# Seven of eight sequences send their tokens to two experts through rows in memory ordered by expert

## The chip, the cores and the metric

The kernel runs on one core of a Trainium2 chip. The core has TensorE (matrix products), VectorE (DVE), ScalarE (ACT), GpSimd (POOL) and SyncE (SP, which only issues transfers here). Each engine works through its own instructions in order and waits on semaphores for the others. The metric is the device time of one execution in microseconds. The kernel before takes 966.37 us, the median of three runs (964.07 to 969.08).

## The reference

The input is x with 8 sequences of 512 tokens of 256 values, all in float32. The first half is an attention of 16 heads plus a memory term, the second a mixture of experts; each is added to its input and normalised.

```python
x = L0_attn_x
x = _layernorm(x + _L0_attn_ref(x, ...), axis=-1)
x = _layernorm(x + _L0_ffn_ref(x, ...), axis=-1)
```

The second half picks for each token the 2 best of 10 experts. Eight are real and two are null (they contribute nothing). The reference computes all eight experts for every token and weighs them, six or more with zero:

```python
gate_probs = jax.nn.softmax(x @ gate_w.T + gate_b, axis=-1)
weights, selected = jax.lax.top_k(gate_probs, 2)
true_weights = weights * (selected < 8)
norm_w = true_weights / where(sum(true_weights) > 0, sum(true_weights), 1)
combine_w = einsum('tk,tke->te', norm_w, one_hot(selected, 10))[:, :8]
expert_out = einsum('td,edh->teh', x, expert_w) + expert_b
out = einsum('te,teh->th', combine_w, expert_out)
```

## The kernel before

A sequence's 512 tokens are four tiles of 128. The program is written out by a planner in Python, before the chip sees it; what the chip executes is a fixed order on every engine.

The backbone is a loop over 32 attention units (sequence b, group g of four heads). Each unit has eight turns. A turn emits score products (`products`, L174): the row maxima need one pass (TensorE L184 and L191, VectorE L194), the scores another (L188), followed by the exponential on ScalarE (L197), a causal selection on GpSimd (L199) and, two turns later, the value products (`values`, L214, TensorE L220). The tile of the maxima's scores has one buffer, so the next one waits until VectorE has reduced the last. A unit begins with the transpose L206.

After its backbone part every turn calls `fill` (L755). It has a credit of TensorE time and spends it on generators: *chains*, which may advance up to twice a turn, and *bulk* work, taken while credit is left. A `yield` of a number is a cost in microseconds; `STEP` goes on at the next turn; `POOL` lets only one chain use GpSimd in a turn; a lambda waits until a condition of the planner holds. All of this is decided while the program is written.

The work put between the attention turns is: the memory term (`lines`, `memory_sums`, until about a third of the span); then for each sequence a front (L597) and its experts (`all_experts`, L691). `prepare` (L551), the first part of a front, loads x again (L558), adds the output's bias and the memory's share on GpSimd, loads the inverted denominators of attention (L571) and multiplies by them (L577). The denominators travel by memory: L230 writes them, L239 reads them in another shape, L243 writes the inverse. `front` then does the output products (L606, L609), the normalisation, the transposes (L629), the gate (L635) and the choice of experts on VectorE with small operations. `all_experts` computes all eight experts for each tile, two at a time:

```python
for k in range(KC):
    nc.tensor.matmul(pe, x1T[:, k, c * P : (c + 1) * P],
                     ws[:, k, 2 * ep : 2 * ep + 2, :].rearrange("p e h -> p (e h)"), ...)   # L707
for e in range(2):
    nc.vector.scalar_tensor_tensor(x1[:, c, :], pe[:, e * D : (e + 1) * D], cw[...], x1[:, c, :], ALU.mult, ALU.add)  # L711
```

Then come the bias by one product (L715), its addition (L716) and the second normalisation, and each tile is stored (L723). Fronts are one chain (`fronts`, L729), so preparation of sequence b+1 starts after front b; a front also waits for experts of earlier sequences (`b < left[0] + 2`, L624), and preparation for a free buffer of x (`b < left[0] + 4`, L552). x transposed lies in on-chip memory for all eight sequences (L85). At the end `fill` is called until everything has been emitted.

Of the kernel before, what the change touches and what calls it, by code (L numbers as in the profile page):

```python
# [27 lines left out]
EARLY, MORE = 0.6, 0.9  # L28
PV, PQ, PO = 1.2, 2.15, (1.05, 0.85, 0.65, 0.45)
ROUNDS = (2, 1, 1, 1)  # L30
AHEAD = 5
HALF = 4
# [35 lines left out]
def block_kernel(ctx, tc, x, xT, wqk, bqk, wtok, wod, memv, memvb, row, gw, we, eb, out):  # L68
# [14 lines left out]
    xt = const.tile([P, B, KC, T], F32, name="xt")  # L83

    def load_xT(b):  # L85
        nc.sync.dma_start(xt[:, b], xT[b].rearrange("(k p) t -> p k t", p=P))
# [4 lines left out]
    load_xT(0)  # L91
# [15 lines left out]
    ebs = const.tile([NTRUE, D], F32, name="ebs")  # L107
# [6 lines left out]
    for b in range(1, B):  # L114
        load_xT(b)
    gws = const.tile([P, KC, NE], F32, name="gws")
    nc.sync.dma_start(gws, gw.rearrange("(k p) e -> p k e", p=P))

# [12 lines left out]
    nc.gpsimd.iota(first, pattern=[[-1, NE]], base=NE, channel_multiplier=0,  # L131
                   allow_small_or_imprecise_dtypes=True)
# [18 lines left out]
    def project_qk(u, w):  # L151


        b, g = UNITS[u]
        pq = bank(f"pq{u}_{w}")
        for k in range(KC):
            nc.tensor.matmul(pq, wq[:, k, w, g // 2, :], xt[:, b, k, :], start=(k == 0), stop=(k == KC - 1))  # L157
        for odd in range(2):
            t = att.tile([P, T], F32, name=f"qk{u + odd}_{w}", tag=f"qk{w}", bufs=4)
            n = NG * w + g + odd  # L160
            nc.scalar.activation(t, pq, AF.Identity, bias=bq[:, n : n + 1], scale=bq[:, 2 * NG + odd : 2 * NG + odd + 1])  # L161
            qk[u + odd, w] = t

    def project_v(b, c):
        pv = bank(f"pv{b}_{c}")
        for k in range(KC):
            nc.tensor.matmul(pv[:, :D], xt[:, b, k, c * P : (c + 1) * P], wt[:, k, CV : CV + D],  # L167
                             start=(k == 0), stop=(k == KC - 1))
        nc.scalar.copy(v_aug[b % 2][:, c, :, 0::2], pv[:, :D].rearrange("p (h q d) -> p h q d", q=2, d=DH))
# [84 lines left out]
    def fold_values():  # L254
# [22 lines left out]
        nc.sync.dma_start(ebs, eb)  # L277
# [6 lines left out]
    def memory():  # L284
        with tc.tile_pool(name="lines", bufs=2) as lp:
            lines_pool.append(lp)
            spawn(memory_factors())
            spawn(fold_values())
            for b in range(B):
                half = b // HALF  # L290
                if b % HALF == 0:


                    t, keep = mem.setdefault(half, {}), memp if half else lp
                    t["rd"] = keep.tile([P, NT, H, HALF, 6], F32, name=f"rd{half}", bufs=1)
                    t["jw"] = keep.tile([P, NT, H, HALF, 7], F32, name=f"jw{half}", bufs=1)
                    t["rn"] = memp.tile([P, NT, H, HALF], F32, name=f"rn{half}", tag="rn", bufs=2)
                    t["gexp"] = memp.tile([P, NT, H, HALF], F32, name=f"gexp{half}", tag="gexp", bufs=2)
                yield lambda: b < 2 or b - 2 in turned
                yield from lines(lp, b)  # L300
            yield lambda: B - 1 in lined and finished.count(0) == 2
        lines_over.append(True)
# [8 lines left out]
    def lines(lp, b):  # L311
# [4 lines left out]
        for c in range(NT):  # L316
            pl = bank(f"pl{b}_{c}")
            for k in range(KC):
                nc.tensor.matmul(pl[:, : CW - CL], xt[:, b, k, c * P : (c + 1) * P], wt[:, k, CL:CW],  # L319
# [180 lines left out]
    def finish(half, h0, rm):  # L500
        yield STEP
        yield lambda: half == 0 or half - 1 in gates
# [48 lines left out]
    def prepare(b):  # L551
        yield lambda: lines_over and b < left[0] + 4  # L552
# [4 lines left out]
        xb = st[b]["xb"] = ff.tile([P, NT, D], F32, tag="x1", name=f"x1_{b}", bufs=4)  # L557
# [39 lines left out]
    def front(b):  # L597

        yield from prepare(b)
        ff, osb, xb = ffp[0], st[b]["osb"], st[b]["xb"]  # L600
        y = xb
        mv = ff.tile([P, NT, 2], F32, tag="mv", name=f"mv1_{b}")
        for c in range(NT):
            pa = bank(f"pa{b}_{c}")
            for k in range(KC):
                nc.tensor.matmul(pa[:, D:], xt[:, b, k, c * P : (c + 1) * P], wt[:, k, CM : CM + D],  # L606
# [8 lines left out]
            yield 1.9  # L615
        yield STEP
        x1 = y
# [6 lines left out]
        yield lambda: b < left[0] + 2  # L624
        x1T = ff.tile([P, KC, T], F32, tag="x1T", name=f"x1T_{b}")
# [28 lines left out]
        for r in range(2):  # L654
# [6 lines left out]
            oh = small(f"oh{r}", NE)  # L661
# [16 lines left out]
        w = small("w", NE)  # L678
        nc.vector.tensor_tensor(w, hot[0], hot[1], ALU.add)
        nc.vector.tensor_tensor(w, w, ex, ALU.mult)  # L680
        yield STEP
        dn = small("dn")
        nc.vector.tensor_reduce(dn, w[:, :, :NTRUE], AX.X, ALU.add)  # L683
        nc.vector.scalar_tensor_tensor(dn, dn, 0.0, dn, ALU.is_equal, ALU.add)
        nc.vector.reciprocal(dn, dn)
        cw = ff.tile([P, NT, NTRUE], F32, tag="cw", name=f"cw_{b}")
        nc.vector.tensor_tensor(cw, w[:, :, :NTRUE], bc(dn, 2, NTRUE), ALU.mult)
        st[b].update(x1=x1, x1T=x1T, cw=cw)
        ready.add(b)

    def all_experts(b):  # L691
# [10 lines left out]
        mv2 = ff.tile([P, NT, 2], F32, tag="mv", name=f"mv2_{b}")  # L702
        for c in range(NT):
# [11 lines left out]
            nc.tensor.matmul(pb[:, :D], cT[:, c * P : (c + 1) * P], ebs, start=True, stop=True)  # L715
# [9 lines left out]

    def fronts():  # L729
        for b in range(B):  # L730
            yield from front(b)

    def tiles():
        for b in range(B):
            yield from all_experts(b)

    left = [0]
# [17 lines left out]
    def fill(need, most=3.0):  # L755
        credit[0] = min(credit[0] + need + (MORE if ready else EARLY), most)
# [22 lines left out]
    for n in range(B // HALF):  # L779
        spawn(memory_ahead(n))  # L780
    spawn(fronts())

    done, credit = set(), [0.0]
    project_qk(0, 0)
# [3 lines left out]
    for u in range(-1, U + 1):  # L788
        b, g = UNITS[u] if 0 <= u < U else (0 if u < 0 else B, -1)
        for i in range(NT if u < U else 2):  # L790
            for pr in range(2):
                products(u, i, pr)
                need = TAKE[i]
# [27 lines left out]
    while chains or any(it[1] != "over" for it in bulk):  # L821
        fill(0.3)
# [60 lines left out]
```

## Time and profile before

| | us |
|---|---|
| median of 3 runs | 966.37 |
| the profiled execution | 966.05 |
| its span, first to last instruction | 964.2 |
| TensorE busy in the span | 885.6 |
| VectorE busy | 606.8 |
| ScalarE busy | 309.6 |
| GpSimd busy | 313.3 |
| start of attention unit 13 | 369.1 |
| start of attention unit 31, the last | 815.7 |

The profile records one execution. Busy times are unions of an engine's instructions; matmuls are pipelined, so their durations overlap and a mean is longer than what one more matmul costs. A float32 product appears as two MATMUL records. The granted clock of TensorE is 0.962 in the mean of the span, and 1.00 in the stretches after 369.1 us until the last 8 us.

### The profile page before, as it was taken

What the parts mean: (1) busy time and instruction counts of PE and PEld (TensorE: products, weight loads), DVE (VectorE), ACT (ScalarE), POOL (GpSimd) and SP (SyncE); (2) the same over time, 40 slices, a digit from 0 to 9 for tenths busy, and PEclk for the clock granted to TensorE, in tenths of its full rate; (3) what the DMA queues carried; (4) which work ended last, traced back from release to release, by engine and by line L of the source; (5) the groups of instructions that cost most, each with busy time, mean ns of one, the idle gap of its engine ahead of it and who ended that gap; (6) DMA issues with size and microseconds to landing.
All of it is one profiled execution on the core that took longest, in us unless ns stands there. A gap on an engine that the chain in (4) does not pass through costs nothing.

```text
span 964.2 us, 14019 instructions
## 1 busy us (share of the span) xinstructions
PE 885.6 (92%) x5360; PEld 426.0 (44%) x5360; DVE 606.8 (63%) x1293; ACT 309.6 (32%) x606; POOL 313.3 (32%) x501
## 2 busy tenths in 40 slices
PE   6999987888788899999999999999999999979996
PEld 3544443444354454354544344543444344334442
DVE  1234657886966656756766866556655676577765
ACT  4164633344324233333323333332333332200000
POOL 1067763536363422521153113211231124230000
PEclk9799988999889799999999999999999999999998
DMA  7300000000000000100100000000000010020000
GB/s 247 95 11 16 11 7 4 3 2 24 4 23 24 13 14 10 39 2 3 39 30 1 2 26 23 23 1 22 28 23 1 4 46 23 3 67 1 22 22 22
DMA packets 25459, 23.67 MB, mean 25 GB/s; under 512 B 8324, under 2 KB 21132, under 8 KB 25392
## 3 DMA queue, kind: packets, MB, share of 16 engines
q1 hardware_dynamic: 24288, 22.22, 7.2%
q8 instruction: 42, 0.69, 0.3%
q10 hardware_dynamic: 1056, 0.40, 0.2%
q0 software_dynamic: 48, 0.16, 0.1%
q14 instruction: 25, 0.20, 0.1%
HBM read 16.73 MB, written 4.73 MB: 22 GB/s over the span
## 4 chain that ended last, share of the span: by engine, by line
PE 69%; DVE 16%; POOL 6%; DMA 3%; issue 3%; ACT 2%; SPq 0%; POOLq 0%; DVEq 0%; ACTq 0%
PE pex L707 22%; PE mx L184 14%; PE po L220 5%; PE pq L157 5%; DVE negmax L194 5%; PE mx L191 4%; PE pa L606 3%; PE pa L609 3%; PE pv L167 2%; PE sc L188 2%; DVE x L711 2%; DMA s<-w 2%; PE pbias L715 2%; PE pm L475 1%; DVE pr L485 1%
## 5 line engine op out<-in xcount | busy, mean ns | idle before, releaser
L197 ACT ACTIVATE pe<-sc 128x1024 f32<-128x1024 f32 (+3 forms) x256 | 180.1, 704 | 415.6 <-PE sc L188 400.0
L194 DVE TENSOR_REDUCE negmax<-mx 128x2 f32<-128x256 f32 (+3 forms) x256 | 209.4, 818 | 154.3 <-PE mx L191 153.9
L184 PE MATMUL mx<-qk,qk 32*128 32x128 f32 (+3 forms) x1024 | 226.7, 500 | 48.3 <-DVE negmax L194 45.8
L199 POOL TENSOR_SCALAR_AFFINE_SELECT pe<-pe 128x256 f32<-128x256 f32 x256 | 104.6, 409 | 475.4 <-ACT pe L197 475.0
L707 PE MATMUL pex<-ws,x1T 128*128 128x512 f32 x512 | 242.1, 606 | 3.7 <-DVE dn L683 2.1
L188 PE MATMUL sc<-qk,qk 32*128 32x512 f32 (+3 forms) x1024 | 217.4, 497 | 2.4 <-ACT pe L197 1.2
L711 DVE SCALAR_TENSOR_TENSOR x<-pex,cw,x 128x256 f32<-128x256 f32 x256 | 123.5, 482 | 92.8 <-PE pex L707 86.8
L184 PEld LDWEIGHTS mx<-qk,qk 32*128 32x128 f32 x1024 | 86.5, 190 | 170.6 <-DVE negmax L194 93.1
L707 PEld LDWEIGHTS pex<-ws,x1T 128*128 128x128 f32 x512 | 90.7, 190 | 112.2 <-issue 104.2
L220 PE MATMUL po<-pe,v_aug 128*32 128x512 f32 (+3 forms) x1024 | 98.9, 459 | 0.0
L188 PEld LDWEIGHTS sc<-qk,qk 32*128 32x128 f32 x1024 | 81.8, 189 | 11.5 <-ACT pe L197 4.7
L191 PEld LDWEIGHTS <-identb 128*128 128x128 bf16 x512 | 29.3, 98 | 119.3 <-issue 112.1
L191 PE MATMUL mx<-mask_ts,identb 128*128 128x128 bf16 x512 | 74.9, 229 | 0.0
L157 PE MATMUL pq<-xt,wq 128*128 128x512 f32 x128 | 65.5, 638 | 5.9 <-DMA xt<-in_xT 5.9
L161 ACT ACTIVATE qk<-pq,bq 128x512 f32<-128x512 f32 x64 | 46.3, 773 | 31.6 <-PE pq L157 31.6
L475 PE MATMUL pm<-ou,dm 128*128 128x144 f32 x256 | 48.4, 320 | 1.6 <-DVE pr L485 1.6
L475 PEld LDWEIGHTS pm<-ou,dm 128*128 128x128 f32 x256 | 39.2, 208 | 17.3 <-issue 12.4
L446 POOL TENSOR_TENSOR ou<-jw,jf 128x288 f32<-128x288 f32 x64 | 43.7, 688 | 1.3
L167 PE MATMUL pv<-wt,xt 128*128 128x256 f32 x128 | 37.9, 423 | 0.0
L585 POOL TENSOR_TENSOR rr_b<-rs_b,half 128x4 f32<-128x4 f32 x8 | 8.1, 1006 | 90.3 <-DVE rs_b L583 90.3
L483 DVE SCALAR_TENSOR_TENSOR ou<-pm,last,ou 32x288 f32<-32x288 f32 x48 | 25.2, 525 | 18.8 <-POOL ou L446 12.8
L319 PE MATMUL pl<-wt,xt 128*128 128x272 f32 x128 | 36.6, 423 | 0.0
(162 smaller groups left out, 872.9 us busy)
## 6 DMA issues: line engine op xcount, KB each, us to landing
xt<-in_xT SPq DMA_DIRECT2D x8, 512.0 KB
x<-in_x SPq DMA_DIRECT2D x8, 512.0 KB
recs<-dr SPq DMA_DIRECT2D x16, 256.0 KB
out_y<-x SPq DMA_DIRECT2D x32, 128.0 KB
ws<-in_we SPq DMA_DIRECT2D x2, 1024.0 KB
s<-w SPq DMA_DIRECT2D x8, 127.0 KB
qk<-nt ACTq DMA_DIRECT2D x32, 8.0 KB
wq<-in_wqk SPq DMA_DIRECT2D x3, 128.0 KB
```

The source lines that it names most:

```text
L157: nc.tensor.matmul(pq, wq[:, k, w, g // 2, :], xt[:, b, k, :], start=(k == 0), stop=(k == KC - 1))
L167: nc.tensor.matmul(pv[:, :D], xt[:, b, k, c * P : (c + 1) * P], wt[:, k, CV : CV + D], start=(k == 0), stop=(k == KC - 1))
L184: nc.tensor.matmul(mx[:, h, :n], qk[m, 0][r, n - P : n], qk[m, 1][r, :n], start=True, stop=False)
L188: nc.tensor.matmul(sc[:, h, :n], qk[v, 1][r, j * P : (j + 1) * P], qk[v, 0][r, j * P :], start=True, stop=True)
L191: nc.tensor.matmul(mx[:, h, n - P : n], identb, mask_ts, start=False, stop=True)
L194: nc.vector.tensor_reduce(negmax[m][:, 2 * pr : 2 * pr + 2, t], mx[:, :, :n], AX.X, ALU.max, negate=True)
L197: nc.scalar.activation(pe[:, :, :n], sc[:, :, :n], AF.Exp, scale=DH**-0.5)
L199: nc.gpsimd.affine_select(out=pe[:, :, :P], in_=pe[:, :, :P], compare_op=ALU.is_ge, fill=0.0, base=0, pattern=[[0, 2], [1, P]], channel_mu ...
L220: nc.tensor.matmul(pos[u][32 * h : 32 * h + 32, j * P :], v_aug[b % 2][:, j, 4 * (g // 2) + h, g % 2 : g % 2 + 2].rearrange("p q d -> p (q ...
L475: nc.tensor.matmul(pm[:, i * HALF * 36 : (i + 1) * HALF * 36], dms[h + i], ou[:, i], start=True, stop=True)
L707: nc.tensor.matmul(pe, x1T[:, k, c * P : (c + 1) * P], ws[:, k, 2 * ep : 2 * ep + 2, :].rearrange("p e h -> p (e h)"), start=(k == 0), sto ...
L711: nc.vector.scalar_tensor_tensor(x1[:, c, :], pe[:, e * D : (e + 1) * D], cw[:, c, 2 * ep + e : 2 * ep + e + 1], x1[:, c, :], ALU.mult, AL ...
```

## The change

For sequences 0 to 6 the experts are no longer computed for all tokens. Each sequence has 1024 choices (two per token). They are given places in a row buffer in device memory, ordered by expert, where each expert's part is rounded up to whole tiles of 128 rows; at most 15 tiles result (8 plus 7 for rounding), and always 15 are worked through.

- `front` keeps, instead of a dense weight matrix, the two one-hot choices (`hot`), the two weights (`wr`), and running counts per expert (`to`, `had`).
- `sort` computes each choice's row: two small TensorE products give ranks and totals, small VectorE operations turn them into tile bases, row numbers `at` (a null expert gets a row past the end), and a table `tab` with the expert of each tile. GpSimd then scatters the tokens by 8 indirect transfers of 128 rows.
- `experts` fetches a tile of sorted rows on SP, transposes it on TensorE with a copy on ScalarE, multiplies by the weights of the expert whose number is loaded from `tab` into registers (for up to 4 tiles at once, on TensorE and VectorE), adds that expert's bias on VectorE, and stores the result to a second row buffer on SP.
- `combine` gathers each token's two result rows by 8 indirect transfers on GpSimd, adds them with their weights, normalises and stores the sequence by one transfer.
- Sequence 7 stays with `all_experts`; its biases are loaded into a small tile, since the biases of all experts now lie spread over 128 partitions.
- x transposed has five buffers; sequences 5 to 7 are loaded when needed, once for the memory's lines and again for attention. Row buffers (three of each kind) are cleared by transfers on SP during the early units.
- Preparation, fronts and reloading are chains of their own. A front waits until the tokens two sequences back have been scattered. The credit per turn after the first front is 0.8 instead of 0.9, and 1.1 instead of 0.3 after attention.

```diff
-EARLY, MORE = 0.6, 0.9
+EARLY, MORE = 0.6, 0.8
+DENSE = 1
+GROUPS = tuple((b,) for b in range(B - DENSE))
+MAXTILES = 8 * max(len(g) for g in GROUPS) + 7
+XT, X1 = 5, 4
...
+    def clear():
...
+        for i in range(3):
+            nc.sync.dma_start(ysl[i][NOROW:], nought[0:1])
+            for rows_of in (xsl[i], ysl[i]):
+                for n in range(0, MAXTILES, 4):
...
+                    nc.sync.dma_start(rows_of[...].rearrange("(n p) d -> p n d", p=P), bc(nought, 1, w))
+                    yield
...
     def front(b):
-        yield from prepare(b)
+        yield lambda: b in prepared and (b < 2 or 'sorted' in group[b - 2])
...
-        yield lambda: b < left[0] + 2
-        x1T = ff.tile([P, KC, T], F32, tag="x1T", name=f"x1T_{b}")
+        x1T = osb
...
+    def sort(p):
...
+        yield lambda: left[0] >= p - 2
+        pr = bank(f"rank{p}")
...
+        nc.tensor.matmul(pr[:, : (n + 1) * NTRUE], ones, gr["had"]..., start=True, stop=False)
+        nc.tensor.matmul(pr[:, : n * NTRUE], ahead, gr["to"]..., start=False, stop=True)
...
+        for c in range(n):
+            yield POOL
+            x1 = gr["x1"][c // NT][:, c % NT, :]
+            for r in range(2):
+                went = nc.gpsimd.indirect_dma_start(
+                    out=xsl[p % 3], out_offset=bass.IndirectOffsetOnAxis(ap=gr["at"][r][:, c : c + 1], axis=0),
+                    in_=x1, in_offset=None, bounds_check=NOROW - 1, oob_is_err=False).ins
...
+    def experts():
...
+                xs[n] = ffp[0].tile([P, D], F32, tag="xs", name=f"xs{p}_{t}", bufs=4)
+                load = nc.sync.dma_start(xs[n], xsl[p % 3][t * P : (t + 1) * P]).ins
...
+                nc.tensor.transpose(pt[:, k * P : (k + 1) * P], xs[n][:, k * P : (k + 1) * P], ident)
+            xT_s[n] = ffp[0].tile([P, KC, P], F32, tag="xTs", name=f"xTs{p}_{t}")
+            nc.scalar.copy(xT_s[n], pt[:, : KC * P]...)
...
+            if t % 4 == 0:
...
+                _, of_t = nc.values_load_multi_w_load_instructions(
+                    group[p]["tab"][0:1, t : t + w], engines=[mybir.EngineType.PE, mybir.EngineType.DVE], ...)
...
+                nc.tensor.matmul(py[:, :D], xT_s[n][:, k, :], ws[:, k, bass.ds(of[n], 1), :]..., ...)
+            ys = ffp[0].tile([P, D], F32, tag="ys", name=f"ys{p}_{t}", bufs=2)
+            nc.vector.tensor_tensor(ys, py[:, :D], ebs[:, bass.ds(of[n], 1), :]..., ALU.add)
+            nc.sync.dma_start(ysl[p % 3][t * P : (t + 1) * P], ys)
+            yield 1.1
...
+    def combine(p):
...
+                    nc.gpsimd.indirect_dma_start(
+                        out=y, out_offset=None, in_=ysl[p % 3],
+                        in_offset=bass.IndirectOffsetOnAxis(ap=gr["at"][r][:, n : n + 1], axis=0))
...
+            nc.sync.dma_start(out[b].rearrange("(c p) d -> p c d", p=P), x1)
+            left[0] += 1
...
     def tiles():
-        for b in range(B):
+        yield from experts()
+        for b in range(B - DENSE, B):
             yield from all_experts(b)
...
     while chains or any(it[1] != "over" for it in bulk):
-        fill(0.3)
+        fill(1.1)
```

## The prediction

> **What bounds the kernel now.** First the page's shares, then the groups of TensorE, then the busy time by stage, then the chain of waits at the end, then single rows of GpSimd.
>
> ```profile
> PE   885.6 (92%) x5360; PEld 426.0 (44%) x5360; DVE 606.8 (63%) x1293; ACT 309.6 (32%) x606; POOL 313.3 (32%) x501
> ...
> L707 PE MATMUL pex<-ws,x1T 128*128 128x512 f32 x512 | 242.1, 606 | 3.7 <-DVE dn L683 2.1
> L711 DVE SCALAR_TENSOR_TENSOR x<-pex,cw,x 128x256 f32<-128x256 f32 x256 | 123.5, 482 | 92.8 <-PE pex L707 86.8
> ```
>
> The experts' products (L707) are TensorE's largest group: 512 MATMUL records, 64 for each of eight sequences (an f32 product is two records). VectorE's adds of their results (L711) wait for TensorE, not the reverse. Next the same by stage; the columns are the stretch, its length, then busy microseconds of each engine.
>
> ```profile
> 42.90:369.10 326.20, 284.27 (x1977) 146.38 (x1976) 209.85 (x385) 135.35 (x298) 167.69 (x262) 0.92 0.04 12
> 369.10:815.70 446.60, 433.33 (x2824) 198.31 (x2822) 290.81 (x632) 149.02 (x249) 121.92 (x196) 1.00 0.06 19
> ```
>
> I cut the span at the 32 transposes L206, which begin an attention unit (four heads of one sequence). Units 13 to 30 fill 369.1 to 815.7 us: 24.8 us each, TensorE busy 97%. There a microsecond of TensorE work is worth nearly a microsecond. Earlier the memory arithmetic also holds TensorE back, and that is not changed. After the last unit begins (815.7), 148.5 us remain. The chain of waits there:
>
> ```profile
> 849.76 3.83 DMA x<-in_x
> ...
> 860.80 3.51 DMA recs<-dr
> ...
> 865.76 0.70 PE pa L609 x2
> 866.46 0.86 PE pa L606 x4
> ...
> 871.64 1.72 PE pex L707 x4
> 873.36 0.62 PE pbias L715 x2
> ...
> 892.24 0.45 PE px L629 x4
> ```
>
> The last front waits for its x, fetched as late as 849.8. These rows also give streaming prices, which I use in place of group means, since pipelined records overlap: a 512-column MATMUL 1.72/4 = 0.43 us, a 256-column one 0.86/4 = 0.215, a transpose 0.45/4 = 0.11, a bias product 0.31.
>
> **The change, part by part.**
>
> *Expert products.* Removed from a sequence: 64 x 0.43 = 27.5, eight bias records x 0.31 = 2.5, eight of L698 about 1.0 (as transposes): 31.0 us. Added: 15 tiles, each 4 records of 256 columns (0.86) and 4 transposes (0.44), so 19.6, and 0.2 for the ranks: 19.8. Net -11.2, for seven sequences **-78 us**. The ideal share of two experts in eight isn't reached: 15 tiles instead of 8, 256 columns instead of 512, and a second transposition. By the order of the changed program's instructions this falls about 2.5 before unit 13, 33 in units 13 to 30, and 43 after.
>
> *Chains of their own.* Preparation no longer stands inside the fronts, so x of sequence 7 is asked for some two units before the end of attention. In the stretch 846 to 866 TensorE is idle about 6 us before single instructions. **-6 us.**
>
> *Register loads.* Each group of up to four tiles loads its experts' numbers into registers of TensorE and VectorE: 28 loads on each, in order, so scores, projections and values queue behind. No row of before shows one. From below: nothing, if TensorE has enough queued work. From above: the Trainium skill, "Runtime: NRT & Kernel Launch", section Instruction fetch mechanics, puts a register load at about 200 ns per register, so an estimate of 0.8 us for four. I take 0.7 exposed: **+20 us**; ends 0 and, with 2 us each, 56. The first load also waits for all engines and most DMA queues: **+3** (near one 512 KB landing, 3.83). Register moves before each product (210) stand behind queued matmuls: 0.
>
> *Scatter and gather.* 16 indirect transfers for each of seven sequences, 112 on GpSimd's queue, in pairs, mostly one pair to a turn of the planner. The nearest row is a plain one of 128 rows:
>
> ```profile
> L95 POOL DMA_DIRECT2D rows<-in_row x1 | 0.8, 752 | 0.8 <-POOLq L871 0.8
> ...
> 747.22 0.41 POOL L199 TENSOR_SCALAR_AFFINE_SELECT pe<-pe 128x256 f32<-128x256 f32 x1 [4.07 <-ACT pe L197]
> 750.46 0.41 POOL L199 TENSOR_SCALAR_AFFINE_SELECT pe<-pe 128x256 f32<-128x256 f32 x1 [2.83 <-ACT pe L197]
> ```
>
> The row says 0.75 us; reading 128 indices comes on top, and I take T = 1.2. Against the change speaks the Trainium skill, "SBUF — State Buffer", section SBUF: two separate sides: a GpSimd DMA of some 620 ns took about 3100 beside a VectorE copy, because descriptors are written through the port pair shared with VectorE. Before has no such transfer beside VectorE work, but shows the lock's other side: a VectorE product of two SBUF operands, (3.6 - 2.2)/7 = 0.2 us in its other seven records, lasts as long as GpSimd's 2.36 us addition beside it.
>
> ```profile
> 853.92 2.22 DVE L680 TENSOR_TENSOR w<-w,ex 128x40 f32<-128x40 f32 x1
> ```
>
> What is queued behind a pair is the next causal selection (L199), and the value products (L220) wait for that. A turn is an eighth of a unit, about 3.05 us after; a pair and a selection take 2T + 0.41. With T = 1.2 that is 2.8 and nothing is late. Above 3.05 it lags in each of four consecutive turns. A selection ends about 4.8 us before its value product begins in this trace (median in units 13 to 30), so a group of four stalls TensorE by 4(2T - 2.64) - 4.8, and some 12 groups lie beside attention. By the row: 0. By the page's 3.1: 9.4 x 12 = 113 us. I take **0**; a gain is excluded, since nothing is removed here.
>
> *Transfers on SP.* 105 tile loads and 105 result stores at 0.33 to 0.45 us of issue: 80 us of SP, which only waits most of the time. A tile is fetched two turns (6 us) ahead, against 3.83 for a 512 KB landing: hidden. But the load of x for sequences 4 to 7 stands behind the store that frees its buffer, and tile transfers queue behind both; result tiles have two buffers, so VectorE would stall and the score maxima with it: 4 x 1.5 = **+6** (0 to 16, a full landing each). Clearing the row buffers (27 transfers, about 12 MB) and reloading three x^T falls where DMA shares are 4%: **+3** (0 to 8).
>
> *VectorE and ScalarE.* VectorE loses 32 x 0.48 + 4 x 0.42 = 17 us per sequence and gains 15 x 0.42 for results, 8 x 0.48 for the sum and some 30 small operations x 0.2: 16. ScalarE gains 15 copies x 0.37 = 5.6. Both stay under TensorE: 0. With less work between them, score products (one buffer) wait more openly for the maxima (1.22 us at full width): 0.25 per unit in 18 units, **+4.5** (0 to 15).
>
> *After attention.* Sequence 6's tiles run with little beside them: transposition, copy (0.37 and some 0.2 of signalling), product in turn, 15 x 0.6 = **+9**. The denominators of sequence 7 pass through four dependent transfers and GpSimd, about 14 us by the rows 845 to 866; only five tiles (6.5 us) lie between, and SP stands still in it: **+8**. The dense sequence, kept last, covers the sum of sequence 6 (8 x 1.2 + some 5 of landing and adds, under 30).
>
> Sum on the profiled span: 964.2 - 78 - 6 + 20 + 3 + 6 + 3 + 4.5 + 9 + 8 = 933.7; with the 1.85 us around it (966.05 - 964.2) 935.6, say **935 us**. The profiled execution agrees with the runs' median (966.37) to 0.3 us.
>
> **The rivals.**
>
> *The stalls are covered* (0.17). If register loads, the barrier, SP's order and the maxima hide (-33.5) and half the exposure after attention (-8.5), the time is 935 - 42 = 893. For it: GpSimd is 32% busy and TensorE always has attention queued. Against it: every queue is in order, and each tile crosses four engines.
>
> *Indirect transfers clog GpSimd* (0.30, slower). Place: the turns of units 13 to 30 with a pair in them. My gain is about 31 us, used up when 12(8T - 15.36) = 31, at T = 2.24. At T = 2.6 the stall is 65 us and the time 1000; at 3.1 it is 1048. For it speaks the page's tripling and the locked VectorE row; against it the 0.75 us of the plain transfer and the 2.8 to 4.1 us of waiting ahead of the selections shown.
>
> *It cancels* (0.08): T near 2.2, or 1.8 us exposed per register load instead of 0.7: 966.
>
> **How the numbers follow.** Mine has 0.45, with its own range 915 to 958 (half of the bounds above on either side). About 0.5% is what a measurement of this kernel can tell from no change. Faster: 0.45 + 0.17 = 0.62; within: 0.08; slower: 0.30. The range of 8 in 10 takes in the rival of covered stalls down to 888 and that of the clogged queue up to 1000 (T = 2.6).
>
> **What would show it.** Right: units 13 to 30 near 24.2 us instead of 24.8 and the stretch after the last unit begins near 117 us instead of 148.5; indirect transfers of 1 to 1.5 us on GpSimd; TensorE's idle time named by register loads. Wrong: value products idle behind GpSimd, transposes idle behind DMA of sorted rows, units longer than 25 us, or VectorE's result adds idle behind their stores.

## The result and the profile after

The changed kernel takes 1018.25 us (median of four runs, 1013.09 to 1033.15) against 965.22 for the kernel before in the same comparison: ratio 1.0566, 95% interval 1.0472 to 1.0661. It is slower by 53 us; I had predicted 935, with 888 to 1000 as the range of 8 in 10. The profile is of the slowest of the four executions (1033.15 us, span 1031.4, 15 us above the median); the same instructions up to unit 31, in a faster execution of the run `busy_tail` below, took 393.2 and 478.2 us where this profile has 392.1 and 486.0.

The page's shares, two clock rows and groups:

```profile
PE 859.4 (83%) x5458; PEld 461.9 (45%) x5458; DVE 596.5 (58%) x1418; ACT 342.4 (33%) x704; POOL 425.4 (41%) x618
PE   6995868788798797897897998897898888888794
...
PEclk9798788999989997998999998899989999767597
...
L880 PE MATMUL py<-ws,xTs 128*128 x420 | 132.8, 450 | 29.0 <-ACT xTs L860 26.5
...
L948 POOL DMA_INDIRECT yg<-ysl,at x56 | 54.8, 979 | 42.7 <-DMA ebk<-in_eb 19.3
...
L824 POOL DMA_INDIRECT xsl<-x,at x56 | 56.0, 1001 | 16.3 <-issue 16.3
```

TensorE fell from 92% to 83% busy in a longer span. Its busy time shrank by only 26 us (885.6 to 859.4): the products are fewer, but the clock row ends in 7, 6, 7, 5, 9, 7 where all but the last slice had 9 before, and a product at half clock counts about double as busy time (four records of L652 below: 1.71 us, then 0.86). The 112 indirect transfers took 1.0 us each; GpSimd, with 41%, is not the bound.

The busy time by stage, columns as before (stretch, length, busy of each engine, granted clock, DMA share, GB/s). The cuts are again the first instruction of unit 13 and of unit 31. The first row is the last stretch of the kernel before, the others are the changed kernel:

```profile
815.70:964.20 148.50, 133.69 (x443) 61.62 (x441) 96.42 (x252) 11.91 (x22) 19.61 (x23) 0.98 0.07 22
...
0.00:392.10 392.10, 319.94 (x2116) 168.61 (x2117) 230.80 (x468) 150.00 (x337) 188.84 (x302) 0.90 0.22 70
392.10:878.10 486.00, 423.00 (x2955) 227.08 (x2954) 294.33 (x737) 173.40 (x323) 193.51 (x268) 0.93 0.25 77
878.10:1031.40 153.30, 116.42 (x393) 66.17 (x391) 71.37 (x214) 19.03 (x45) 43.02 (x49) 0.74 0.30 92
```

All three stretches are longer than before (369.1, 446.6 and 148.5 us), also the first, where almost no expert work lies. Units 13 to 30 take 27.0 us instead of the 24.2 predicted. TensorE is busy 87% there, at a clock of 0.93 instead of 1.00.

A stretch can be split: its length is the time TensorE stood idle, plus its work at full clock, plus half of the time it was busy while the clock was halved (such work takes twice its time). From the records of matrix products and of the granted clock (whose only values are 1.0 and 0.5), in us:

| | length | idle | busy at half clock | work at full clock |
|---|---|---|---|---|
| before: to unit 13 | 369.1 | 50.5 | 59.6 | 288.8 |
| before: units 13 to 30 | 446.6 | 13.3 | 3.4 | 431.6 |
| before: from unit 31 | 148.5 | 14.8 | 0.0 | 133.7 |
| after: to unit 13 | 392.1 | 72.2 | 69.4 | 285.2 |
| after: units 13 to 30 | 486.0 | 63.0 | 63.9 | 391.0 |
| after: from unit 31 | 153.4 | 36.9 | 55.8 | 88.5 |

The work fell by 3.6 + 40.6 + 45.2 = 89 us. Idle time rose by 93.5 and the halved clock added (189.1 - 63.0)/2 = 63 us. 93.5 + 63 - 89 = 67, the difference of the spans.

What TensorE waited for, in the view of waits of the changed kernel (us in total, times, longest):

```profile
PE mx L220 <- DVE negmax L230: 54.2, 59, 5.1
...
PE py L880 <- ACT xTs L860: 26.5, 35, 3.3
...
PE pxs L858 <- DMA xs<-xsl: 21.0, 15, 3.7
...
PE pl L359 <- DMA xt<-in_xT: 17.5, 3, 9.0
```

The maxima were the largest wait before too (45.8). New are the copy of the transposed tile (`xTs`), the sorted tile itself (`xs`), and the reloaded x^T (`xt`). The causal selection, my dangerous rival's place, has 4.8 us in all. SP's issues beside the longest x^T wait, and TensorE there, from the timeline (start, duration, engine, line):

```profile
81.98 6.67 SPq L368 DMA_DIRECT2D s<-w  x1
88.70 0.42 SPq L95 DMA_DIRECT2D xt<-in_xT  x1
...
92.65 1.28 PE L359 MATMUL pl<-wt,xt 128*128 128x272 f32 x2 [9.01 <-DMA xt<-in_xT]
```

SP stands 6.67 us in a transfer of one row (0.8 KB) for the memory term (`s<-w`), the reload of x^T can be issued only then, and TensorE goes on 3.9 us after that. The row itself is not the load: what the DMA engines move from 82.9 to 90.3 us are 511 packets of 256 bytes, and 508 of them make up the 127 KB transfer issued just ahead (L367, `s<-w` too). They go out one after another at 18 ns each, with 8% of the 16 engines busy from 83.0 to 88.6 us. That SP stands because of them is the likeliest reading and was not tried; other one-row transfers (L137, 1 KB to memory) took 0.24 to 0.33 us. Before, the same transfers stood in the same queue, with nothing urgent behind them. In the units, the copy to `xTs` shares ScalarE with attention:

```profile
484.31 1.02 ACT L233 ACTIVATE pe<-sc 128x1024 f32<-128x1024 f32 x1
485.21 0.59 ACT L265 COPY raw<-po 128x512 f32<-128x512 f32 x1
...
487.36 0.29 DVE L284 TENSOR_SCALAR sm<-sm 128x256 f32<-128x256 f32 x1
...
487.68 0.42 ACT L285 ACTIVATE sm<-sm 128x256 f32<-128x256 f32 x1 [1.88 <-DVE sm L284]
...
488.01 0.63 ACT L860 COPY xTs<-pxs 128x256 f32<-128x256 f32 x2
```

The transposes ended at 485.16. ScalarE took the exponential and the copy of `raw`, then stood 1.88 us for an exponential of the memory gate whose operand VectorE still had to make; the copy was queued behind it, and TensorE's next product waited 3.25 us. After the last unit the chain of waits reads:

```profile
930.88 0.45 SPq L883
931.43 4.57 DMA xs<-xsl
936.13 0.68 PE pxs L858 x2
937.31 2.08 PE py L880 x4
939.38 1.71 PE pa L652 x4
...
942.22 0.86 PE pa L652 x4
```

The tile is asked for behind a result store on SP, lands 4.6 us later, and its four records then take 2.08 us instead of 0.86. The clock is halved until 941.5 us, as the same four records of L652 on either side of it show.

### The profile page after: what moved, and what is told of

It reads as the page before. It is cut to its first block, busy times and chain, and to the rows that moved or that the text cites. A ratio compares the mean times of both kernels' runs of the same rounds, so it can differ in the third digit from the quotient of the medians.

```text
span 1031.4 us, 15647 instructions
## 1 busy us (share of the span) xinstructions
PE 859.4 (83%) x5458; PEld 461.9 (45%) x5458; DVE 596.5 (58%) x1418; ACT 342.4 (33%) x704; POOL 425.4 (41%) x618
## 3 DMA queue, kind: packets, MB, share of 16 engines
q1 hardware_dynamic: 67062, 64.18, 19.8%
## 4 chain that ended last, share of the span: by engine, by line
PE 56%; DVE 17%; DMA 8%; issue 6%; POOL 5%; ACT 4%; SPq 2%; another core or an unknown queue 0%; DVEq 0%; ACTq 0%; POOLq 0%
PE mx L220 14%; PE py L880 10%; PE po L256 5%; DVE negmax L230 5%; PE pq L193 4%; DMA xs<-xsl 4%; PE mx L227 3%; PE pa L652 3%; PE pa L655 3%; PE pxs L858 3%; PE pl L359 2%; PE pv L203 2%; DMA s<-w 2%; PE sc L224 2%; PE pg L681 2%
## 5 line engine op out<-in xcount | busy, mean ns | idle before, releaser
L220 PE MATMUL mx<-qk,qk 32*128 32x128 f32 (+3 forms) x1024 | 230.6, 514 | 57.7 <-DVE negmax L230 54.2
L224 PE MATMUL sc<-qk,qk 32*128 32x512 f32 (+3 forms) x1024 | 226.9, 518 | 4.7 <-ACT pe L233 3.0
L880 PE MATMUL py<-ws,xTs 128*128 x420 | 132.8, 450 | 29.0 <-ACT xTs L860 26.5
L880 PEld LDWEIGHTS py<-ws,xTs 128*128 128x128 f32 x420 | 84.1, 220 | 57.6 <-ACT xTs L860 38.2
L882 DVE TENSOR_TENSOR ys<-py,ebs 128x256 f32<-128x256 f32 x105 | 43.7, 421 | 111.0 <-PE py L880 97.4
L948 POOL DMA_INDIRECT yg<-ysl,at x56 | 54.8, 979 | 42.7 <-DMA ebk<-in_eb 19.3
L860 ACT COPY xTs<-pxs 128x256 f32<-128x256 f32 x105 | 38.1, 373 | 99.0 <-PE pxs L858 93.4
L858 PE MATMUL pxs<-ident,xs 128*128 128x128 f32 x210 | 46.1, 316 | 23.7 <-DMA xs<-xsl 21.0
L824 POOL DMA_INDIRECT xsl<-x,at x56 | 56.0, 1001 | 16.3 <-issue 16.3
L359 PE MATMUL pl<-wt,xt 128*128 128x272 f32 x128 | 42.2, 474 | 17.5 <-DMA xt<-in_xT 17.5
L858 PEld LDWEIGHTS pxs<-ident,xs 128*128 128x128 f32 x210 | 25.7, 156 | 58.2 <-issue 35.1
```

The lines of the kernel that those rows point to most:

```text
L220: nc.tensor.matmul(mx[:, h, :n], qk[m, 0][r, n - P : n], qk[m, 1][r, :n], start=True, stop=False)
L224: nc.tensor.matmul(sc[:, h, :n], qk[v, 1][r, j * P : (j + 1) * P], qk[v, 0][r, j * P :], start=True, stop=True)
L359: nc.tensor.matmul(pl[:, : CW - CL], xl[b][:, k, c * P : (c + 1) * P], wt[:, k, CL:CW], start=(k == 0), stop=(k == KC - 1))
L824: went = nc.gpsimd.indirect_dma_start(out=xsl[p % 3], out_offset=bass.IndirectOffsetOnAxis(ap=gr["at"][r][:, c : c + 1], axis=0), in_=x1, ...
L858: nc.tensor.transpose(pt[:, k * P : (k + 1) * P], xs[n][:, k * P : (k + 1) * P], ident)
L880: nc.tensor.matmul(py[:, :D], xT_s[n][:, k, :], ws[:, k, bass.ds(of[n], 1), :].rearrange("p e h -> p (e h)"), start=(k == 0), stop=(k == K ...
```

## The experiments

The theory after the result: the products saved are real, but (a) the reload of x^T behind SP's slow transfers delays the first stretch, (b) sorted tiles come just in time through SP, TensorE and ScalarE, so that TensorE idles in units and after them, and (c) each such wait lets the clock fall. Rivals: the prepared chains and reloads alone are to blame, not the sorting; the register loads; or the saved work is not worth its time on this kernel, whatever the sorting costs. The ratios below are to runs of the kernel before on the same chip.

### The scaffolding without sorting

`all_dense`: the changed program with all eight sequences dense, no sorting and no clearing; chains of their own and reloads stay, with the kernel before's credits and buffers of x1T.

```diff
-EARLY, MORE = 0.6, 0.8
+EARLY, MORE = 0.6, 0.9
...
-DENSE = 1
+DENSE = 8
...
-        x1T = osb
+        yield lambda: b < left[0] + 2
+        x1T = ff.tile([P, KC, T], F32, tag="x1T", name=f"x1T_{b}")
...
-    cleared = clear()
+    cleared = iter(())
```

> All eight sequences keep the dense experts (nothing is scattered, cleared or gathered), but x^T comes by need and preparation, fronts and reloading are chains of their own, with the credits of before. If the loss lies in the sorted tiles (my theory): unit 13 begins 10 to 25 us later than before because the reloads of x^T wait on SP behind a slow transfer, the rest is as before or 5 us better, total 965 to 990. If the chains of their own are what costs: units 13 to 30 take 460 us or more and the total is above 1000.

Measured: 993.03 us, ratio 1.0296 (1.0247 to 1.0344). The stretches are 385.3, 457.4 and 150.4 us: +16, +11 and +2. About half of the loss comes with the part of the change that saves nothing; most of it before unit 13, where TensorE waits 15.9 us for x^T. The 11 us in the units are mostly the clock (23.9 us busy at half clock instead of 3.4); why it fell there is not shown, nor was this run repeated with the reload on another queue. The -6 us that I had counted for own chains didn't appear.

### The reload on another queue

`xl_act`: only the three reloads of x^T move, from SP's queue to ScalarE's.

```diff
-        nc.sync.dma_start(to[b], xT[b].rearrange("(k p) t -> p k t", p=P))
+        (queue or nc.sync).dma_start(to[b], xT[b].rearrange("(k p) t -> p k t", p=P))
...
-                    load_xT(b + 1, lp, xl, bufs=1)
+                    load_xT(b + 1, lp, xl, queue=nc.scalar, bufs=1)
```

> As the changed kernel, but the three reloads of x^T for the memory's lines are issued from ScalarE's queue instead of SP. If they were late because SP stands 6 to 8 us in the one-row transfer of the lines ahead of them: unit 13 begins at 375 us or earlier instead of 392, and the total falls by 12 to 20 us. If the clearing transfers fill the DMA engines instead: the waits of the lines for x^T stay above 12 us in sum and the total falls by less than 5.

Measured: 992.84 us, ratio 1.0283 (1.0213 to 1.0354): 25 us less than the changed kernel. Unit 13 begins at 367.4 us (392.1 in the changed kernel, 369.1 before), and in that stretch the view of waits has

```profile
PE pl L359 <- DMA xt<-in_xT: 2.2, 1, 2.2
```

instead of 17.5. Units 13 to 30 stay at 486.0. So (a) is settled: it was SP's order, not bandwidth, since the clearing transfers stayed as they were.

### Sorted tiles further ahead

`ahead2`: tiles are fetched four ahead instead of three, and turned up to two ahead; for the space one more x^T is reloaded.

```diff
-XT, X1 = 5, 4
+XT, X1 = 4, 4
...
-            fetch(n + 3)
+            fetch(n + 4)
...
-            if n + 1 < len(row) and there(n + 1):
-                turned(n + 1)
-                yield 0.4
+            for nn in range(n + 1, min(n + 3, len(row))):
+                if nn not in xT_s and there(nn):
+                    turned(nn)
+                    yield 0.4
```

(and six and four buffers for the tiles `xs` and `xTs`.)

> As the changed kernel, but sorted tiles are fetched four ahead instead of three (six buffers) and transposed up to two ahead instead of one (four buffers); for the space x^T has four buffers instead of five. If short slack in the tile's chain stops TensorE: its waits for the copies and for the sorted rows fall from 48 us together to under 20, the half-clock time falls with them, and the total falls by 20 to 50 us. If the lack of TensorE work itself lowers the clock: waits fall, the half-clock time stays above 180 us, and the total falls by less than 15.

Measured: 1008.51 us, ratio 1.0512 (1.0423 to 1.0602), not distinguishable from the changed kernel in total. In the profile units 13 to 30 fell to 458.2 us and the wait for the copy from 26.5 to 9.8 us; the wait for sorted tiles stayed (22.7), the wait for the maxima rose from 54.2 to 66.6 us, and the first stretch, with the fourth reload, got 4 us longer. Of the 48 us of waits for copies and tiles 32.5 were left, not the under 20 that my theory asked for.

### The clock after the last unit

`busy_tail`: from unit 31 on, ten small bf16 products (some 0.06 us each) ahead of each sorted tile's product, to keep TensorE busy; nothing reads their result (`late` is filled when unit 31 begins).

```diff
+            for _ in range(10 if late else 0):
+                nc.tensor.matmul(py[:, D : D + P], identb, mask_ts, start=True, stop=True)
```

> As the changed kernel, but from the last attention unit on each sorted tile is preceded by ten small bf16 products into unused columns of its bank (0.066 us each at full clock, about 18 us of added TensorE work over 28 tiles). If the halved clock of TensorE is what makes the stretch after attention long: half-clock time there falls from 68 us to under 35 and the stretch from 153 us to 145 or less. If it is the latency of the tiles' chain: the stretch stays or grows by up to 20 us.

Measured: 1016.5 us, ratio 1.056 (1.0506 to 1.0614). After the last unit TensorE did 18 us more work at full clock (106.4 instead of 88.5), and yet the stretch took 141.2 us instead of 153.4; busy time at half clock fell from 55.8 to 9.7. In `xl_act`, where this stretch's program is the same as in the changed kernel, it took 147.4, so about half of the 12 us is spread between executions. Set against `xl_act`, 17 us of work came in, 8 us of idle time went, and 15 us of time lost to the clock went too ((40.2 - 9.7)/2). So the halved clock is real time, and work that kept it up paid for itself in that stretch; the total, 1016.5 us, is that of the changed kernel.

### Mending the feed, step by step

`both`: the reloads on ScalarE's queue and tiles further ahead, together.

> The changed kernel with two things: the reloads of x^T issue from ScalarE's queue (three of them become four, since the sorted tiles need room), and sorted tiles are fetched four ahead into six buffers and turned up to two ahead into four. If the early loss is the reload behind SP's transfers and the middle loss is the sorted tile coming just in time, both gains add: unit 13 starts near 368 us, units 13 to 30 take near 458, the last stretch near 147, so 970 to 985 us. If the two compete (more transfers in the same queues), it is 990 or more. If rows by expert were right and only the feeding wrong, it would go below 965; I doubt it, since the clock stays low where the TensorE has less work.

Measured: 992.64 us, ratio 1.0248 (1.0177 to 1.0319). The gains didn't add: it equals `xl_act`. The four reloads cost 9 us in the first stretch (376.0 against 367.4), the units gained 19 (467.0 against 486.0), the end lost 5, within what executions differ. My expectation missed.

`both_xs_act`: on top of it, loads of sorted tiles from ScalarE's queue.

```diff
-                load = nc.sync.dma_start(xs[n], xsl[p % 3][t * P : (t + 1) * P]).ins
+                load = nc.scalar.dma_start(xs[n], xsl[p % 3][t * P : (t + 1) * P]).ins
```

> As the run with both, and the loads of the sorted tiles are issued by ScalarE too, so that they no longer stand behind result stores that wait for the VectorE on SP. If SP's order is what is left of the idle time: transposes wait for sorted tiles under 8 us in all (about 22 in the changed kernel), 10 to 20 us less than the run with both. Rival: ScalarE, which issues in order, stands at a load whose buffer is not free, and the exponentials behind it come late: as long or longer.

Measured: 979.4 us, ratio 1.0127 (1.0072 to 1.0182). The transposes' wait for sorted tiles is gone from the view of waits (23.7 us in `both`), and the time fell by 13: the tile loads had stood behind result stores that wait for VectorE. But the wait for the maxima in units 13 to 30, 13.0 us in the changed kernel, now reads

```profile
PE mx L220 <- DVE negmax L230: 26.9, 25, 3.9
```

`both_dense2`: on top of `both`, two dense sequences instead of one (`DENSE = 2`, two buffers of `cw`).

> As the run with both, and two sequences (6 and 7) instead of one take all experts densely. Work: 14 dense products per tile instead of four, about 11 us more TensorE work at full clock, but nothing of the last rows waits for a row in memory. If the end is lost to idle time and clock: last stretch within 3 us of the run with both or shorter. If only the count of products matters: about 11 us longer in total.

Measured: 985.17 us, ratio 1.0205 (1.015 to 1.026). The end took 146.6 us with 106.7 us of work, against 152.2 with 92.3 in `both`. TensorE did 14 us more and ended no later; the total is lower by 7 with overlapping intervals.

`both_more`: on top of `both`, `MORE` 1.0 instead of 0.8.

> As the run with both, with the expert work that a unit may take raised from 0.8 to 1.0 of a unit's allowance. If the order puts too little expert work beside the attention units, so that the tensor engine idles and its clock halves: units 13 to 30 stay as long and the end is 5 to 15 us shorter. If the sorted work is limited by when rows are there: no difference within 5 us.

Measured: 979.11 us, ratio 1.0126 (1.0071 to 1.0181). The end shrank by 27 us, the units grew by 9: better than I had expected, as 17 us of work went from the end to where more lies beside it.

`best_more1`: `both` with the loads of sorted tiles on ScalarE's queue and `MORE` 1.0.

> All that helped, in one kernel: reloads of x^T and loads of sorted tiles from ScalarE's queue, four tiles ahead, turned two ahead, and 1.0 instead of 0.8 of expert work per unit. The last two measured -13 each on the same base; if they add, 965 to 970 us, level with the kernel before. If they share one idle time, 975 to 980.

Measured: 971.64 us, ratio 1.0088 (1.0055 to 1.0121). Of the two gains' 27 us 21 add up, or 1.6 of 2.4% by the ratios, each of which is to its own chip.

`best_more2`: the same with `MORE` 1.2.

> As the run before, with 1.2. If expert work beside attention keeps the TensorE busy and its clock up, 5 to 10 us less again; if the softmax's own chain is now held by copies and stores in front of it, the units grow by as much as the end shrinks: within 3 us.

Measured: 989.34 us, ratio 1.0284 (1.0243 to 1.0326). Worse by 18, which neither branch of the expectation had: in the profiled executions units 13 to 30 went from 474.1 to 486.8 us at the same work (404.4 and 403.6), with 59.9 us idle instead of 46.8.

`best_dense2`: `best_more1` with two dense sequences.

> As the run best_more1, with sequences 6 and 7 dense. On the earlier base this gave -7 us, with 11 us more TensorE work in the end. If the end is bound by the chain from row to product, again 5 to 10 less; if more expert work beside the units has already filled it, 0 to 10 more.

Measured: 968.92 us, ratio 1.004 (1.0011 to 1.0068), the best of the sorted kernels that compute the reference, and still not below the kernel before. TensorE waits 64.9 us for the maxima in it (54.2 in the changed kernel) and 3.1 for copies (26.5): what was taken from the feed came back in part as waits for VectorE.

### Register loads

`best_noreg`: `best_more1` without register loads; the expert of a tile is fixed in the program, so tokens get other experts than they ask for (lines shortened; the bias on VectorE likewise).

```diff
-                _, of_t = nc.values_load_multi_w_load_instructions(...)
+                of_t = [(t + i) % NTRUE for i in range(w)]
...
-ws[:, k, bass.ds(of[n], 1), :]
+ws[:, k, of[n] : of[n] + 1, :]
```

> As the run best_more1, without the loads of expert numbers into registers: tile t takes expert t mod 8, fixed in the program, so the products are of other experts than the tokens asked for, with the same count and shape. If the register loads cost what I predicted (0.7 us each, 28 times), 20 us less. If they cost what their records show (0.33 us on the TensorE, 0.35 on the VectorE), at most 9 us, and less where the engine would have waited anyway: 0 to 9.

Measured: 966.27 us, ratio 1.0023 (0.9998 to 1.0048), 5 us below `best_more1` (1.0055 to 1.0121). The register loads, with the register moves ahead of the products, cost about 5 us, not 20. In the changed kernel they read (ns: least, median, most):

```profile
L874 PEldq TENSOR_LOAD <-tab x28: 328/333/777, 424.2 to 975.6; - x28
L874 DVEq TENSOR_LOAD <-tab x28: 341/347/1737, 427.0 to 978.3; - x28
```

### Less work without sorting

The mended kernel only came level. So the other side: take about as many products from the kernel before, with none of the sorting; the sums then lack experts and are not the reference's. `before_half` leaves out two of four products of expert pairs for seven sequences (28 tiles of 2 x 4 records x 0.43 = 96 us), `before_3of4` one.

```diff
-            for ep in range(NTRUE // 2):
+            for ep in range(NTRUE // (4 if b < B - 1 else 2)):
```

> The kernel before, with two of the four products of expert pairs left out for seven sequences, and with them their two times two additions on the VectorE: about the count of products that sorting leaves, with none of the sorting (experts 5 to 8 are missing from these sums). If less TensorE work is worth what my sum says, 965 - 78 = about 887 us. If the clock follows the work down and the other engines take over, half of it or less is gained: 920 to 940. If work removed here is worth nothing at all, within 5 us of 965.

> The same with one of the four left out (experts 7 and 8 missing). Halfway between the kernel before and the run with two left out if each product removed is worth the same; if the clock is lost from some amount of missing work on, more than half of the gain is already here.

Measured: 929.3 us, ratio 0.9647 (0.9616 to 0.9677), and 934.09, ratio 0.9701 (0.9661 to 0.9742). The first 48 us removed gave 27 us, the next 48 only 5, with intervals that touch. Stages of `before_half`:

```profile
0.00:372.60 372.60, 319.08 (x2097) 165.25 (x2098) 220.40 (x413) 148.55 (x335) 172.04 (x282) 0.91 0.11 32
372.60:836.20 463.60, 425.20 (x2794) 197.19 (x2793) 292.04 (x648) 152.31 (x254) 128.72 (x202) 0.95 0.07 21
836.20:937.00 100.80, 73.02 (x249) 35.62 (x247) 44.75 (x121) 9.59 (x17) 13.14 (x18) 0.78 0.05 17
```

Units 13 to 30 became *longer*, 463.6 instead of 446.6 us, with 26 us less work (405.2 instead of 431.6): idle time rose from 13.3 to 38.4 and busy time at half clock from 3.4 to 40.1. 25 + 37/2 - 26 = 17. The wait for the maxima in these units, before and in `before_half`:

```profile
PE mx L184 <- DVE negmax L194: 12.1, 20, 1.2
...
PE mx L184 <- DVE negmax L194: 33.6, 40, 2.5
```

The order was the next suspect: the credit 0.9 lets a turn take expert work as soon as there is some, so that later turns have none. `before_half_06` and `before_half_12` change only it:

```diff
-EARLY, MORE = 0.6, 0.9
+EARLY, MORE = 0.6, 0.6
```

> As the run before_half (929), with 0.6 instead of 0.9 of expert work per turn, so that less work is spread over more turns. If the units 13 to 30 became longer with less work because the order spends the work in bursts and then has none, this evens it out: that stretch below 450 us (it was 464) and the total under 920. If the units are held by the maxima's own chain whenever little else is there, the stretch stays near 460 and work moves behind the last unit: 930 to 945.

> The same with 1.2. If the tail is what is left to shorten, more work beside the units: total 3 to 10 us below 929. If bursts are the trouble, longer than 929.

Measured: 894.88 us, ratio 0.9247 (0.9207 to 0.9288), with 0.6; 926.37, ratio 0.9573 (0.9524 to 0.9622), with 1.2. The stages with 0.6:

```profile
0.00:366.60 366.60, 314.78 (x2090) 163.72 (x2091) 217.56 (x407) 148.56 (x335) 171.02 (x281) 0.91 0.11 33
366.60:785.40 418.80, 394.21 (x2749) 185.33 (x2747) 268.60 (x597) 150.38 (x252) 123.27 (x200) 0.98 0.07 21
785.40:892.30 106.90, 91.42 (x303) 42.49 (x301) 61.79 (x179) 10.17 (x19) 17.79 (x21) 0.90 0.08 26
```

With 0.6 the same removal gives 71 of its 96 us: units of 23.3 us at a clock of 0.98. One number of the order decides between 32 and 71.

The records of units 13 to 30, counted by turn (from one turn's first mask product L191 to the next's, 142 turns), show where TensorE idles: in turns without an expert product. Before, 76 turns have none and hold 12.4 of the 13.3 us of idle time; in `before_half` 102 turns hold 35.7 of 38.4; with 0.6 it is 104 turns and 23.1 of 24.6. So 0.6 did not leave fewer bare turns. It broke up their longest row, from 21 in a row to 11, and the idle time of one fell from 0.35 to 0.22 us. Bursts are not the whole account, though: with 1.2 there are three rows of 23 bare turns, and yet the time did not rise above 929 as I had expected. Nor was 0.6 tried with all the products in place, so that part of the 71 us may be the credit's own.

`best_even06` and `best_even07` set `MORE` to 0.6 and 0.7 in `best_dense2`.

> As the run best_dense2 (969), with 0.6 instead of 1.0 of expert work per turn. In the kernel before with half of its products that credit was worth 34 us. If the sorted kernel loses by bursts too: units 13 to 30 go from 472 to about 440, 25 us of work move behind the last unit: 950 to 962, below the kernel before. If its losses are single waits in the sorted chain, the work only moves to the end: 970 to 985.

> The same with 0.7: between the two, 955 to 965 if bursts are the trouble, 968 to 978 if single waits are.

Measured: 1007.16 us, ratio 1.0455 (1.0384 to 1.0525), and 989.0, ratio 1.0219 (1.0137 to 1.03). The sorted kernel is not mended that way. In `best_even06` units 13 to 30 did fall to 436.8 us (from 471.6 in `best_dense2`), but with 50 us less work in them, and the end grew to 195.1; over the span TensorE idles 151 us and is busy at half clock 133 (`before_half_06`: 92 and 87.5), and VectorE, which reduces the maxima, stands for the result tiles' stores:

```profile
DVE ys L883 <- DMA ysl<-ys: 25.8, 9, 7.1
```

In `best_dense2` that wait is 5.1 us. That the missing gain of the sorted kernel lies in this one wait was not tried (more buffers for result tiles, or their stores on another queue). What can be said: with another credit, the removed work alone is worth some 71 of its 97 us. `best_dense2` has 77 us less work than the kernel before (777.3 instead of 854.1 by the same split); at that rate some 56 us should have come, and it is 5 us slower. So sorting, with the chains and reloads that come with it, still costs it about 60 us, an estimate; which part of the sorting, stays open.

## Why the prediction was wrong

The step that failed is the one from work to time. On the profiled span the sum said -78 of work and +47.5 for all waits and stalls (with the -6 for own chains), and had no term for the clock; measured were -89 of work, +93.5 of idle time and +63 for the halved clock. Those differences, -11, +46 and +63, are the 98 us between 933.7 and 1031.4.

*Expert products (-78).* Near in size and place: the work fell by 89 us, 40.6 of it in units 13 to 30 (predicted 33) and 45.2 after (43). Part of that is luck: I priced four transposes for a sorted tile, and the profile has two (L858, 210 records for 105 tiles), so the sum by my own prices would have been about -101. Wrong was the sentence that carried it into time, "there a microsecond of TensorE work is worth nearly a microsecond". With the order as it was, the first 48 us removed without any sorting were worth 27 and all 96 us 32: idle time rose by 41 us in `before_half`, 24 of them in waits for the maxima, and the clock took another 29.

*No term for the clock.* The profile of before showed the clock halving before unit 13 (59.6 us busy at half clock), where TensorE idles. I named only its mean per stage and took the 1.00 of the later stages as fixed. It cost (189.1 - 63.0)/2 = 63 us of the profiled span. The clock's records in the changed kernel lie on a grid of 3.41 us. In the windows of that grid just before its 29 falls to half clock TensorE was idle for a median of 1.9 us, mostly in one gap (median 1.8). Windows that stayed at full clock held 1.5 us at most after the first 10 us, but three falls followed windows with only 0.9 to 1.1, so the idle time of one window does not decide alone. Counted by gap at full clock, 22 of 24 gaps of 1.5 us or more had a fall within 3.4 us after them, and 4 of 22 gaps of 1.0 to 1.5 us; in `xl_act` 18 of 26, and 2 of 18. The Trainium skill, "TensorE: Matmul & The Clock Gate", Part 1, speaks of an idle window of about 3.4 us before the clock halves. By that reading few of these waits would matter (2 of 29 windows were idle throughout); by the trace, a wait of 1.5 to 2.5 us was mostly enough.

*Clearing and reloading (+3, 0 to 8).* The first loss in time: "falls where DMA shares are 4%" argued from bandwidth where the queue's order decided. The reload stood behind transfers in which SP stands 6.4 to 8.1 us, and unit 13 started 23 us late; another queue returned 25 us. The trace of before has the eight transfers with that duration:

```profile
L328 SPq DMA_DIRECT2D s<-w x8: 6433/6484/6829, 39.0 to 125.8; - x8
```

*Transfers on SP (+6).* Right that tile transfers queue behind others, wrong about which: I had x behind its store and "hidden" for the tile loads, two turns ahead. They stood behind result stores that wait for VectorE, and TensorE waited 21.0 us for tiles; on the base of `both`, moving the tile loads to another queue returned 13 us. SP's wait:

```profile
SPq L883 <- DVE ys L882: 229.7, 70, 10.5
```

*ScalarE's copies (+9 after attention, 0 inside).* Inside the units I counted the copy's duration, not its place in ScalarE's order: 19.8 us of TensorE's waits for them lie in units 13 to 30, 6.8 after the last unit begins. The sorted tiles' own waits after attention (9.0) came on top.

*Register loads (+20).* Mis-sized: 0.33 us each and 5 us in all. No row of before showed one, and the estimate from the Trainium skill, "Runtime: NRT & Kernel Launch", Instruction fetch mechanics (0.8 us for four registers), was over twice too high. *The barrier of the first load (+3):* at 424.2 us products run without a gap beside it: 0.

*Scatter and gather (0).* Right: 1.0 us each (I took 1.2), 4.8 us of waits at the value products. The rival of a clogged GpSimd, which held all my chance of "slower", is refuted. That the kernel is slower, as this rival would have had it, came by another way. What the Trainium skill, "SBUF — State Buffer", SBUF: two separate sides, tells of a transfer beside a VectorE copy (some 620 to 3100 ns, five times as long and not the "tripling" of my prediction) is not seen for these transfers: 19 of the 112 lay at least 95% beside VectorE work, with a median of 0.97 us against 0.98 for the 33 with under 20% beside it, and the longest of all took 1.29.

*Own chains (-6)* did not show: the last stretch of `all_dense` isn't shorter. *The maxima (+4.5):* sized for units 13 to 30, where the wait was 13.0 us instead of 12.1; 7.5 more arose before unit 13. It grew there in the runs with tiles further ahead (26.9 us in `both_xs_act`, 26.8 in `both_more`). *The denominators (+8):* TensorE's waits after unit 31 begins have none for them: 0.

Of what the prediction said would show it wrong, two signs appeared: transposes idle behind the DMA of sorted rows (21.0 us), and units longer than 25 us (27.0). The other two, value products behind GpSimd and result adds behind their stores, came to 4.8 and 3.6 us.

## What to carry to other kernels

Before work is taken off the busiest engine, ask what that engine will wait for in its place and whether the written order will spread what is left; leaving out about the same work without the machinery around it, with the order's settings tried again, tells in a few runs what it is worth (here 32 us, then 71). A transfer that is newly urgent has to be placed by what stands ahead of it in its queue, with the durations of those issues, not by the share of bandwidth in use. Gaps of 1.5 us or more on TensorE were mostly followed by a fall to half clock here (22 of 24, 18 of 26), the shortest of them 3.4 us long, and that time belongs in the sum.

## What was not expected of the hardware

SP stood 6.4 to 8.1 us in a transfer of one row (0.8 KB) while the 127 KB transfer ahead of it went out in packets of 256 bytes, one after another; 128 KB and 512 KB transfers were issued in 0.3 to 0.5 us (medians of a line). A scatter or gather of 128 rows took 0.98 to 1.0 us of GpSimd, with VectorE 58% busy. A load of up to four registers took 0.33 us on TensorE. And 18 us of added small products did not lengthen the last stretch, while its time at half clock fell from 55.8 to 9.7 us.
